# Layer 3 of a four-layer network on one core: one half's products summed by TensorE, the other half's by VectorE, in an order planned without the exclusion of VectorE and GpSimd

## The chip, the core and the metric

The kernel runs on one core of a Trainium2 chip. The metric is the time of one execution in device microseconds (us). A core has a matrix engine (TensorE, PE in the profile; PEld is its weight load), a vector engine (VectorE, DVE), an engine for functions of one input (ScalarE, ACT), a general engine (GpSimd, POOL) and one that issues transfers (SyncE, SP). Each engine works through its own queue in order. Engines wait for one another by semaphores, and an instruction that waits holds up all that stand behind it in its queue. SBUF is the large on-chip memory; PSUM is the small one that TensorE writes, in eight banks of 128 x 512 float32.

## The reference: what is computed

Four layers follow each other on x of 8 x 256 x 32 x 32. The change is in the last one, layer 3, a deformable convolution. Cut to what matters:

```
h = silu(bn(conv2d(x, w_cv1, 3x3)))              # 256 -> 128 channels
t = gelu(layernorm(depthwise3x3(h) + b_dw))
value  = h @ w_inp + b_inp
offset = t @ w_off + b_off                        # 4 groups x 9 taps x (x, y)
mask   = softmax(t @ w_msk + b_msk, over 9 taps)
o = sum over 9 taps of mask * bilinear(value at tap + offset)
out = x + silu(bn(o @ w_out + b_out))
```

As long as no offset is larger than 1, each bilinear sample of a 3 x 3 tap lies in a 5 x 5 window. So o is a sum of 25 products: the value image shifted by (sx, sy), times a weight for every pixel and group. The kernel computes these 25 weights a pixel from offsets and mask, forms the 25 products and adds them.

## The kernel before

Layer 3 works batch by batch, b = 0 to 7, each in two halves h of 512 pixels (16 rows of 32), channels on the 128 partitions. A tile of one half is 128 x 512 float32, one PSUM bank.

The front of a batch: `add_normed` (L1174) finishes the layer ahead of it in x, `border` copies it into a padded image, `convolve3` (L1182) does 18 float32 matmuls a half into one PSUM tile `pc`, `silu` (L1187) puts them in the image `h3`. `values` and `values_copy` make the value image `v3`. `depthwise` (L1205 on ScalarE, then eight multiply-adds in PSUM at L1208 on VectorE) and the layer norm (`centered`, `variances`, `deviations`, `inverse` at L1240, `inverse_spread`, `scaled` at L1250) lead to `gelu`, `offsets3` and `offsets3_add` (L1266). `masks` is the softmax: a maximum, a subtraction (L1300), an exponential on ScalarE, a sum and reciprocal, a multiplication (L1307). `weights` (L1319 to L1325) builds the 25 weights of each pixel in 15 instructions, on GpSimd for b > 0 and on VectorE for b = 0. `parts` (L1334, L1336) splits them into three bfloat16 parts, ScalarE casting and VectorE subtracting; TensorE turns them and ScalarE copies them to `wT`.

The sum of a half, 25 steps s: `shift_weights` (L1355) spreads one step's weights over the channels by a matmul into one of three PSUM tiles `pw`. `product` (L1360) multiplies it by the shifted value image on VectorE into one of six SBUF tiles `pr`. Each product is then added by one of two engines: `add_pe` (L1366) adds it in the PSUM tile `pa` by a matmul with the identity, and `add_pool` (L1372 and L1374) adds it in the SBUF tile `part` on GpSimd. `by_pe` (L1131) gives TensorE steps 1, 5, 9, 13, 17 and 21 for b < 4 and the twelve odd steps up to 23 for b >= 4; GpSimd has the rest. `add_both` (L1377) adds the two sums on VectorE, `outward` (L1381) and `outward_silu` (L1386) are the last matmul and the activation, `add_input` (L1391) adds x on GpSimd, and `store` issues the transfer out.

The order of the work is planned while the program is written out. Every step is a `piece` with an engine, a planned duration, a rank, the pieces it follows, and the rings from which it takes a buffer and to which it gives one back. `Order.run` repeatedly picks, over all engines, the piece that can start first by the planned times, the lower rank on a tie, and emits it. So the plan decides in which order each engine's queue holds the pieces; on the chip only data and buffers are waited for. A ring's buffer comes free 0.15 us after the planned end of the piece that gives it. Front pieces have rank 100 b, convolutions 100 b + 100, products and their adds 100 b + 150.

One ring, `port`, has one entry and no buffer. Every GpSimd piece but one (the clearing of the weights' tile) takes and gives it, and so do the VectorE pieces L1300, L1307 and L1334: in the plan these never overlap a GpSimd piece, and two GpSimd pieces stand at least 0.15 us apart. Planned durations are 0.68 for a product, 0.86 for a TensorE add, 1.25 for a GpSimd add, 0.45 for each of L1300 and L1307, 1.0 for L1334, and 0.75, 2.1 and three times 0.75 for each third of the weights on GpSimd.

Of the kernel before, what the change touches and what calls it, by code (L numbers as in the profile page):

```python
# [8 lines left out]
F32 = mybir.dt.float32  # L9
# [9 lines left out]
P = 128  # L19
# [3 lines left out]
HALF = N // 2  # L23
# [62 lines left out]
def pixels(ap):  # L86
    return ap.rearrange("c (r w) -> c r w", w=W)
# [71 lines left out]
def conv_seq_kernel(ctx: ExitStack, tc: tile.TileContext, d: dict, out: bass.AP):  # L159
    nc = tc.nc  # L160
    x_in = d["x"]
    B = x_in.shape[0]
# [10 lines left out]
    ident = const.tile([P, P], F32, name="ident")  # L173
# [62 lines left out]
    with ExitStack() as s0:  # L236
        w = s0.enter_context(tc.tile_pool(name="a_w", bufs=1))
# [419 lines left out]
    with ExitStack() as s1_:  # L657
# [58 lines left out]
        def piece(key, engine, time, rank, after, f, *args, take=(), give=(), lag=Order.LAG):  # L716
            T[key] = work.add(engine, time, rank, [T[a] for a in after if a in T], lambda: f(*args), take, give, lag)
# [349 lines left out]
    with ExitStack() as s3_:  # L1067
# [55 lines left out]
        def bank3():  # L1123
# [4 lines left out]
        nc.vector.tensor_reduce(group, ident.rearrange("p (g c) -> p g c", c=GC), AX.X, ALU.add)  # L1128


        by_pe = [range(1, 25, 4) if b < 4 else range(1, 25, 2) for b in range(B)]  # L1131
        by_pool = [[s for s in range(25) if s not in by_pe[b]] for b in range(B)]

        work = Order(
            port=1, ld=3, xp0=1, xp1=1, h3=3, v3=2, ln=1, wt=1, wT=2, pr=6, part=2, res=3, spread=2,
            ps=2, pc=1, pd=1, pw=3, pa=1,  # L1140
        )
        T, S = {}, {}

        def piece(key, engine, time, rank, after, f, *args, take=(), give=(), lag=Order.LAG, kind=None, port=False):
            if port:
                take, give = [*take, "port"], [*give, "port"]
            T[key] = work.add(engine, time, rank, [T[a] for a in after if a in T], lambda: f(*args), take, give, lag, kind)

        def cols(h):
# [205 lines left out]
            nc.tensor.matmul(S["pw", b, h, s], sel[: rows(i), r, :], S["wT", b][: rows(i), i, cols(h)], start=True, stop=True)  # L1355

        def product(b, h, s):
            S["pr", b, h, s] = gp.tile([P, HALF], F32, name="pr")
            v = window(v3s[b % 2], s // 5, s % 5, H // 2, h * H // 2)
            nc.vector.tensor_mul(pixels(S["pr", b, h, s]), pixels(S.pop(("pw", b, h, s))), v)  # L1360

        def add_pe(b, h, s):
            on_pe = by_pe[b]
            if s == on_pe[0]:
                S["acc", b, h] = pa.tile([P, HALF], F32, name="pa")
            nc.tensor.matmul(S["acc", b, h], ident, S.pop(("pr", b, h, s)), start=s == on_pe[0], stop=s == on_pe[-1])  # L1366

        def add_pool(b, h, n):
            on_pool = by_pool[b]
            if n == 1:  # L1370
                S["part", b, h] = two.tile([P, HALF], F32, name="part")
                nc.gpsimd.tensor_add(S["part", b, h], S.pop(("pr", b, h, on_pool[0])), S.pop(("pr", b, h, on_pool[1])))  # L1372
            else:
                nc.gpsimd.tensor_add(S["part", b, h], S["part", b, h], S.pop(("pr", b, h, on_pool[n])))  # L1374
# [25 lines left out]
        for b in range(B):  # L1400

            r = 100 * b
            for t in range(2):
                piece(("ld", b, t), "SP", 0.5, r, [], load, b, t, take=["ld"], lag=5.0)
                for h in range(2):
                    piece(("n", b, t, h), "ACT", 0.75, r, [("ld", b, t)], normed3, b, t, h, take=["ps"], give=["ld"] * h)
                    piece(("a", b, t, h), "DVE", 0.68, r, [("n", b, t, h)], add_normed, b, t, h, give=["ps"])
                piece(("xp", b, t), "ACT", 1.08, r, [("a", b, t, 0), ("a", b, t, 1)], border, b, t, take=[f"xp{t}"])
            last = ("c", b - 1, 1, 1, 8)
            for h in range(2):  # L1410
                for t in range(2):
                    for k in range(9):
                        c = b, h, t, k
                        take = ["pc"] if t == k == 0 else []
                        give = [f"xp{t}"] if h == 1 and k == 8 else []
                        piece(("c", *c), "PE", 0.86, r + 100, [("xp", b, t), last], convolve3, *c, take=take, give=give)
                        last = "c", *c
                piece(("si", b, h), "ACT", 0.78, r, [last], silu, b, h, take=["h3"] * (1 - h), give=["pc"], kind="silu")
            for h in range(2):
# [12 lines left out]
            piece(("inv", b), "DVE", 1.74, r, [("dev", b)], inverse, b)  # L1432
            for h in range(2):
                piece(("is", b, h), "PE", 0.86, r, [("inv", b)], inverse_spread, b, h, take=["ps"])
                piece(("sc", b, h), "DVE", 0.68, r, [("is", b, h), ("zc", b, h)], scaled, b, h, give=["ps"])
                piece(("ge", b, h), "ACT", 0.68, r, [("sc", b, h)], gelu, b, h, kind="gelu")
                piece(("o", b, h), "PE", 1.1, r, [("ge", b, h), ("o", b, h - 1)], offsets3, b, h, take=["ps"] + ["wt"] * (1 - h), give=["ln"] * h)
                piece(("oa", b, h), "DVE", 0.6, r, [("o", b, h), ("oa", b, h - 1)], offsets3_add, b, h, give=["ps"])
            om = [("oa", b, 0), ("oa", b, 1)]
            piece(("ms", b, 0), "DVE", 0.7, r, om, masks, b, 0)  # L1440
            piece(("ms", b, 1), "DVE", 0.45, r, [("ms", b, 0)], masks, b, 1, port=True)
            piece(("ms", b, 2), "ACT", 0.44, r, [("ms", b, 1)], masks, b, 2, kind="exp")
            piece(("ms", b, 3), "DVE", 1.0, r, [("ms", b, 2)], masks, b, 3)
            piece(("ms", b, 4), "DVE", 0.45, r, [("ms", b, 3)], masks, b, 4, port=True)
            for i in range(3):
                piece(("ha", b, i), "ACT", 0.67, r, om + [("ha", b, i - 1)], hats, b, i)
            piece(("ha", b, 3), "DVE", 0.72, r + 90, [("ha", b, 0)], hats, b, 3)
# [4 lines left out]
            for i in range(3):  # L1452
                for j in range(-1, 4):
                    time = (0.75, 2.1, 0.75, 0.75, 0.75)[j + 1] if b else (0.4, 1.06, 0.47, 0.47, 0.47)[j + 1]
                    piece(("w", b, i, j), "POOL" if b else "DVE", time, r, ready + last, weights, b, i, j, port=True)
                    last = [("w", b, i, j)]
            for i in range(3):
                piece(("p", b, i, 0), "ACT", 0.86, r, last, parts, b, i, 0)
                last = [("p", b, i, 0)]
                if i < 2:  # L1460
                    piece(("p", b, i, 1), "DVE", 1.0, r, last, parts, b, i, 1, port=True)
                    last = [("p", b, i, 1)]
            for i in range(3):
                piece(("t", b, i), "PE", 1.0, r, last + [("t", b, i - 1)], turned3, b, i, take=["ps"], give=["wt"] if i == 2 else [])
# [2 lines left out]
            r = 100 * b + 150  # L1467
            for h in range(2):
                k = b, h
                for s in range(25):  # L1470
                    last = s == 24 and h == 1
                    before = ("g", *k, s - 1) if s else ("g", b, 0, 24) if h else ("g", b - 1, 1, 24)
                    after = [("tc", b, s // SB), before] + ([("sel", s % SB, 2)] if b == h == 0 else [])
                    piece(("g", *k, s), "PE", 0.25, r, after, shift_weights, *k, s, take=["pw"], give=["wT"] if last else [])
                    piece(("pr", *k, s), "DVE", 0.68, r, [("g", *k, s), ("vc", b, 0), ("vc", b, 1)], product, *k, s, take=["pr"], give=["pw"] + ["v3"] * last)
                on_pe, on_pool = by_pe[b], by_pool[b]
                for s in on_pe:
                    after = [("pr", *k, s)] + ([("ap", *k, s - on_pe.step)] if s > on_pe[0] else [])
                    piece(("ap", *k, s), "PE", 0.86, r, after, add_pe, *k, s, take=["pa"] if s == on_pe[0] else [], give=["pr"])
                for n in range(1, len(on_pool)):  # L1480
                    after = [("pr", *k, on_pool[n])] + [("pr", *k, on_pool[0]) if n == 1 else ("ao", *k, n - 1)]
                    piece(
                        ("ao", *k, n), "POOL", 1.25, r, after, add_pool, *k, n,
                        take=["part"] if n == 1 else [], give=["pr"] * (1 + (n == 1)), port=True,
                    )
                piece(("ab", *k), "DVE", 0.68, r - 100, [("ap", *k, on_pe[-1]), ("ao", *k, len(on_pool) - 1)], add_both, *k, give=["pa"])
                for t in range(2):
                    piece(("ow", *k, t), "PE", 0.86, r - 100, [("ab", *k)], outward, *k, t, take=["ps"], give=["part"] * t)
                    piece(("os", *k, t), "ACT", 0.78, r - 50, [("ow", *k, t)], outward_silu, *k, t, take=["res"], give=["ps"], kind="silu")
                    piece(("oi", *k, t), "POOL", 1.25, r - 100, [("os", *k, t)], add_input, *k, t, port=True)  # L1490
# [6 lines left out]
        ps = bank3()  # L1497
# [248 lines left out]
```

## Time and profile before

| | |
|---|---|
| median of 3 runs | 4257.02 us (4256.65 to 4259.13) |
| the profiled execution | 4256.73 us |
| its span, first to last instruction | 4254.9 us |
| mean granted TensorE clock | 0.977 |
| busy, of the span | PE 93%, DVE 71%, POOL 78%, ACT 44% |
| layer 3's stage, about 3570 to 4255 us | PE 608.3, DVE 470.7, POOL 462.6, ACT 245.2 us busy |
| products of batch 0 to 7 begin at | 3665, 3745, 3818, 3894, 3969, 4052, 4133, 4195 us |
| last convolution of batch 0 to 7 ends at | 3609, 3649, 3710, 3772, 3839, 3902, 3966, 4079 us |

How to read it: the page gives each engine's busy time, the span in 40 slices (each digit the busy share in tenths), and groups of instructions by line of the program, written out<-in with their shapes. In a group, "x400 | 258.0, 683 | 105.7 <-PE pw L1355 61.3" means 400 instructions, busy for 258.0 us, 683 ns each on average, with 105.7 us of idle time of the engine just before them, 61.3 of which were ended by TensorE's `pw`. A row of an order of time gives start, length, the instruction, how many in a row, and in brackets the idle time before it and what ended it. A row of a single line gives shortest, median and longest duration in ns. A row of stretches gives the stretch, its length, each engine's busy time with its number of instructions, the granted clock, and the transfers' share and rate. A float32 matmul stands as two rows in the trace.

### The profile page before, as it was taken

How to read it: one execution, taken by the hardware profiler on the slowest of the kernel's cores; microseconds unless marked ns; L12 is line 12 of the kernel's file. 1: busy time of each engine (PE TensorE's matmuls, PEld its weight loads, DVE VectorE, ACT ScalarE, POOL GpSimd, SP SyncE). 2: the span in 40 equal slices, each digit the busy share in tenths (PEclk: the TensorE clock that was granted, in tenths of full speed). 3: DMA queues.
4: the chain of work that ended last, by engine and by line, in shares of the span. 5: the costliest groups of instructions: out<-in, count | busy, mean ns of one | idle time of the engine just before them, and what ended most of it. 6: DMA issues, size and time to landing. Idle time of an engine off the chain costs nothing.

```text
span 4254.9 us, 60310 instructions
## 1 busy us (share of the span) xinstructions
PE 3972.3 (93%) x20975; PEld 1542.8 (36%) x20975; DVE 3026.9 (71%) x5147; ACT 1858.0 (44%) x3335; POOL 3313.3 (78%) x2023
## 2 busy tenths in 40 slices
PE   6999999999999999999999999898899978999976
PEld 2333333333333333333333333343343333444432
DVE  6767777777777767777677776567777774777665
ACT  2555545545545555555555555332232324443321
POOL 2888889889898898888888889357777771489767
PEclk8999999999999999999999999999999998999998
DMA  5212212212222222122222121134344442000000
GB/s 174 62 54 57 77 50 63 71 50 65 66 56 69 59 59 73 51 65 68 53 60 74 51 62 48 45 99 115 116 120 121 121 132 72 5 11 15 15 15 21
DMA packets 207225, 283.11 MB, mean 67 GB/s; under 512 B 87216, under 2 KB 117440, under 8 KB 206656
## 3 DMA queue, kind: packets, MB, share of 16 engines
q1 hardware_dynamic: 176352, 195.46, 16.2%
q0 software_dynamic: 28720, 77.90, 6.2%
q10 hardware_dynamic: 1840, 5.81, 0.4%
q8 instruction: 169, 2.77, 0.3%
q14 instruction: 144, 1.18, 0.1%
HBM read 181.07 MB, written 63.82 MB: 58 GB/s over the span
## 4 chain that ended last, share of the span: by engine, by line
PE 72%; DVE 13%; POOL 7%; issue 4%; DMA 3%; ACT 2%; SPq 0%; DVEq 0%; POOLq 0%; ACTq 0%
PE av L460 20%; PE pb L403 12%; PE sc L448 11%; PE pb L386 5%; PE pc L1182 5%; POOL g L885 5%; PE pb L534 3%; PE pa L1366 2%; PE pb L330 2%; PE pm L752 2%; PE po L765 2%; DMA g<-table,idx 2%; DVE pm L407 2%; PE pw L1355 2%; DVE r L491 1%
## 5 line engine op out<-in xcount | busy, mean ns | idle before, releaser
L470 POOL TENSOR_TENSOR esum<-esum,e 128x1024 f32<-128x1024 f32 x762 | 1809.0, 2407 | 55.1 <-ACT e L449 54.7
L407 DVE TENSOR_REDUCE pm<-pb 128x1 f32<-128x512 f32 x2016 | 1356.3, 685 | 656.1 <-PE pb L403 652.0
L449 ACT ACTIVATE e<-sc 128x512 f32<-128x512 f32 x2048 | 1056.5, 603 | 677.0 <-PE sc L448 665.7
L460 PE MATMUL av<-e,v 128*64 128x512 f32 x4096 | 1054.2, 593 | 0.0
L403 PE MATMUL pb<-sk,sq 128*64 128x512 bf16 x4032 | 773.2, 387 | 56.3 <-DVE x L542 23.5
L885 POOL DMA_INDIRECT g<-table,idx x576 | 550.4, 955 | 256.4 <-issue 159.0
L403 PEld LDWEIGHTS <-sq 128*64 128x64 bf16 x4032 | 266.7, 109 | 911.5 <-issue 887.0
L448 PE MATMUL sc<-q,k 32*128 32x512 f32 x4096 | 590.6, 641 | 0.0
L468 POOL TENSOR_TENSOR esum<-e 128x1024 f32<-128x1024 f32 x127 | 303.2, 2409 | 298.9 <-ACT e L449 298.9
L460 PEld LDWEIGHTS av<-e,v 128*64 128x64 f32 x4096 | 295.0, 137 | 208.1 <-issue 117.3
L1374 POOL TENSOR_TENSOR part<-part,pr 128x512 f32<-128x512 f32 x224 | 289.4, 1293 | 67.5 <-DVE pr L1360 56.2
L1360 DVE TENSOR_TENSOR pr<-pw,v 128x512 f32<-128x512 f32 x400 | 258.0, 683 | 105.7 <-PE pw L1355 61.3
L1182 PE MATMUL pc<-xpad,wc 128*128 128x512 f32 x576 | 279.0, 611 | 4.1 <-ACT h L1187 4.1
L448 PEld LDWEIGHTS sc<-q,k 32*128 32x128 f32 x4096 | 164.6, 183 | 229.8 <-issue 185.6
L534 PE MATMUL pb<-o,wp 128*64 128x512 f32 x1024 | 244.3, 596 | 1.4 <-DVE r L512 1.2
L752 PE MATMUL pm<-y,wide 128*128 128x512 f32 x512 | 237.9, 609 | 6.1 <-DVE y L726 5.7
L386 PE MATMUL pb<-wide,y 128*64 128x256 f32 x2048 | 241.8, 379 | 0.0
L765 PE MATMUL po<-hid,w 128*128 128x512 f32 x512 | 239.7, 615 | 1.8 <-DVE x L769 1.7
L491 DVE RECIPROCAL r<-r 128x128 f32<-128x128 f32 x252 | 237.1, 942 | 0.1
L390 ACT COPY v<-pb 128x512 f32<-128x512 f32 x128 | 74.9, 585 | 266.0 <-PE pb L386 266.0
L907 DVE TENSOR_TENSOR near_p<-g,near_p 128x320 f32<-128x320 f32 (+1 forms) x384 | 177.3, 462 | 13.2
L911 DVE TENSOR_TENSOR samp<-samp,near_p 128x320 f32<-128x320 f32 (+1 forms) x384 | 174.0, 453 | 13.2
(256 smaller groups left out, 3893.7 us busy)
## 6 DMA issues: line engine op xcount, KB each, us to landing
sq<-lev_d SPq DMA_DIRECT2D x512, 64.0 KB
r<-r SPq DMA_DIRECT2D x504, 64.0 KB
sk<-lev_d SPq DMA_DIRECT2D x496, 64.0 KB
lev_d<-lev SPq DMA_DIRECT2D x180, 128.0 KB
u_d<-u SPq DMA_DIRECT2D x60, 256.0 KB
g<-table,idx POOLq DMA_INDIRECT x576, 2.7
table<-v SPq DMA_DIRECT2D x32, 256.0 KB
out<-res SPq DMA_DIRECT2D x32, 256.0 KB
```

Source lines behind the costliest of these rows:

```text
L386: nc.tensor.matmul(ps[c * 64 : (c + 1) * 64, (mt % 2) * 256 : (mt % 2 + 1) * 256], ys[b][:, t, k0 : k0 + 64], wv[:, t, g * 256 : (g + 1) * ...
L403: nc.tensor.matmul(ps[c * 64 : (c + 1) * 64, :], sq[pair][:, c, q0 : q0 + 64], sk[pair][:, c, kh * HALF : (kh + 1) * HALF], start=True, st ...
L407: nc.vector.tensor_reduce(maxima[m][:, pair, qt, kh : kh + 1], ps, AX.X, ALU.max)
L448: nc.tensor.matmul(ps, k[r, kt * P : (kt + 1) * P], q[r, h * HALF : (h + 1) * HALF], start=True, stop=True)
L449: nc.scalar.activation(es[m, kt, j // 2][:, j % 2, :], ps, AF.Exp)
L460: nc.tensor.matmul(av[i * HD : (i + 1) * HD, :], vss[b, g][:, kt, j * HD : (j + 1) * HD], e[:, i, :], start=kt == 0, stop=kt == NT - 1,)
L470: eng.tensor_add(sums[m, pair], sums[m, pair], es.pop((m, kt, pair)))
L534: nc.tensor.matmul(ps[c * 64 : (c + 1) * 64, :], wp[:, 2 * g + i, o0 : o0 + 64], outs[(b, g, h), i], start=i == 0, stop=i == 1,)
L752: nc.tensor.matmul(ps, w1[:, t, i * P : (i + 1) * P], ys[b, h][:, t, :], start=t == 0, stop=t == 1)
L765: nc.tensor.matmul(pss["o", b, h, t], w2[:, j, t * P : (t + 1) * P], hids[b, h, j], start=j == 0, stop=j == 7)
L885: nc.gpsimd.indirect_dma_start(out=g[:, k, :], out_offset=None, in_=tables[b][:TR, :], in_offset=bass.IndirectOffsetOnAxis(ap=idxs[b][:, t ...
L1182: nc.tensor.matmul(S["c", b, h], wc[:, t, k, :], tap(xpads[t], k, H // 2, h * H // 2), start=t == k == 0, stop=t == 1 and k == 8,)
```

## The change

It touches layer 3 alone.

- For batches 0 to 5 the first half's products are summed by TensorE (8 of 25) and GpSimd (17), the second half's by VectorE (10) and GpSimd (15). For batches 6 and 7 TensorE has 12 in both halves, as before.
- In a half that VectorE helps, the first helped product (step 1) is written straight into the PSUM tile `pa`, which it takes then, and nine more are added to it by VectorE in place, one float32 tensor_tensor each.
- The ring `port` is gone. The planned durations of L1300 and L1307 become 0.8, that of L1334 becomes 1.7.
- The VectorE pieces L1174, L1250 and L1266 get rank r - 500; VectorE's adds have one less than the products' rank. The convolution's rank, `r + 100`, is written `100 * b + 100`, which is the same number there.

The diff, cut where a line only loses `port=True`:

```diff
-        by_pe = [range(1, 25, 4) if b < 4 else range(1, 25, 2) for b in range(B)]
-        by_pool = [[s for s in range(25) if s not in by_pe[b]] for b in range(B)]
+        HELP = [("PE", 8), ("DVE", 10)] * 6 + [("PE", 12)] * 4
+        helper = {(b, h): HELP[2 * b + h][0] for b in range(B) for h in range(2)}
+        helped = {(b, h): [(2 * i + 1) * 25 // (2 * HELP[2 * b + h][1]) for i in range(HELP[2 * b + h][1])] for b in range(B) for h in range(2)}
+        by_pool = {k: [s for s in range(25) if s not in helped[k]] for k in helped}
...
         work = Order(
-            port=1, ld=3, xp0=1, xp1=1, h3=3, v3=2, ln=1, wt=1, wT=2, pr=6, part=2, res=3, spread=2,
+            ld=3, xp0=1, xp1=1, h3=3, v3=2, ln=1, wt=1, wT=2, pr=6, part=2, res=3, spread=2,
             ps=2, pc=1, pd=1, pw=3, pa=1,
         )
...
-            if port:
-                take, give = [*take, "port"], [*give, "port"]
...
         def product(b, h, s):
-            S["pr", b, h, s] = gp.tile([P, HALF], F32, name="pr")
+            on = helped[b, h]
+            if s == on[0] and helper[b, h] == "DVE":
+                dst = S["acc", b, h] = pa.tile([P, HALF], F32, name="pa")
+            else:
+                dst = S["pr", b, h, s] = gp.tile([P, HALF], F32, name="pr")
             v = window(v3s[b % 2], s // 5, s % 5, H // 2, h * H // 2)
-            nc.vector.tensor_mul(pixels(S["pr", b, h, s]), pixels(S.pop(("pw", b, h, s))), v)
-
-        def add_pe(b, h, s):
-            on_pe = by_pe[b]
-            if s == on_pe[0]:
+            nc.vector.tensor_mul(pixels(dst), pixels(S.pop(("pw", b, h, s))), v)
+
+        def add_helper(b, h, s):
+            on = helped[b, h]
+            if helper[b, h] == "DVE":
+                nc.vector.tensor_add(S["acc", b, h], S["acc", b, h], S.pop(("pr", b, h, s)))
+                return
+            if s == on[0]:
                 S["acc", b, h] = pa.tile([P, HALF], F32, name="pa")
-            nc.tensor.matmul(S["acc", b, h], ident, S.pop(("pr", b, h, s)), start=s == on_pe[0], stop=s == on_pe[-1])
+            nc.tensor.matmul(S["acc", b, h], ident, S.pop(("pr", b, h, s)), start=s == on[0], stop=s == on[-1])
...
-                    piece(("a", b, t, h), "DVE", 0.68, r, [("n", b, t, h)], add_normed, b, t, h, give=["ps"])
+                    piece(("a", b, t, h), "DVE", 0.68, r - 500, [("n", b, t, h)], add_normed, b, t, h, give=["ps"])
...
-                        piece(("c", *c), "PE", 0.86, r + 100, [("xp", b, t), last], convolve3, *c, take=take, give=give)
+                        piece(("c", *c), "PE", 0.86, 100 * b + 100, [("xp", b, t), last], convolve3, *c, take=take, give=give)
...
-                piece(("sc", b, h), "DVE", 0.68, r, [("is", b, h), ("zc", b, h)], scaled, b, h, give=["ps"])
+                piece(("sc", b, h), "DVE", 0.68, r - 500, [("is", b, h), ("zc", b, h)], scaled, b, h, give=["ps"])
...
-                piece(("oa", b, h), "DVE", 0.6, r, [("o", b, h), ("oa", b, h - 1)], offsets3_add, b, h, give=["ps"])
+                piece(("oa", b, h), "DVE", 0.6, r - 500, [("o", b, h), ("oa", b, h - 1)], offsets3_add, b, h, give=["ps"])
...
-            piece(("ms", b, 1), "DVE", 0.45, r, [("ms", b, 0)], masks, b, 1, port=True)
+            piece(("ms", b, 1), "DVE", 0.8, r, [("ms", b, 0)], masks, b, 1)
...
-            piece(("ms", b, 4), "DVE", 0.45, r, [("ms", b, 3)], masks, b, 4, port=True)
+            piece(("ms", b, 4), "DVE", 0.8, r, [("ms", b, 3)], masks, b, 4)
...
-                    piece(("p", b, i, 1), "DVE", 1.0, r, last, parts, b, i, 1, port=True)
+                    piece(("p", b, i, 1), "DVE", 1.7, r, last, parts, b, i, 1)
...
-                    piece(("pr", *k, s), "DVE", 0.68, r, [("g", *k, s), ("vc", b, 0), ("vc", b, 1)], product, *k, s, take=["pr"], give=["pw"] + ["v3"] * last)
-                on_pe, on_pool = by_pe[b], by_pool[b]
-                for s in on_pe:
-                    after = [("pr", *k, s)] + ([("ap", *k, s - on_pe.step)] if s > on_pe[0] else [])
-                    piece(("ap", *k, s), "PE", 0.86, r, after, add_pe, *k, s, take=["pa"] if s == on_pe[0] else [], give=["pr"])
+                    piece(
+                        ("pr", *k, s), "DVE", 0.68, r, [("g", *k, s), ("vc", b, 0), ("vc", b, 1)], product, *k, s,
+                        take=["pa" if dve and s == on[0] else "pr"], give=["pw"] + ["v3"] * last,
+                    )
+                for i, s in list(enumerate(on))[dve:]:
+                    after = [("pr", *k, s)] + ([("ap" if i > dve else "pr", *k, on[i - 1])] if i else [])
+                    piece(
+                        ("ap", *k, s), "DVE" if dve else "PE", 0.7 if dve else 0.86, r - dve, after, add_helper, *k, s,
+                        take=[] if dve or s > on[0] else ["pa"], give=["pr"],
+                    )
```

More of the change, by code (lines that the diff above doesn't have):

```diff
@@ L1142, in conv_seq_kernel, with piece @@
         T, S = {}, {}
-        def piece(key, engine, time, rank, after, f, *args, take=(), give=(), lag=Order.LAG, kind=None, port=False):
-            if port:
-                take, give = [*take, "port"], [*give, "port"]
+        def piece(key, engine, time, rank, after, f, *args, take=(), give=(), lag=Order.LAG, kind=None):
             T[key] = work.add(engine, time, rank, [T[a] for a in after if a in T], lambda: f(*args), take, give, lag, kind)
@@ L1357, in product @@
         def product(b, h, s):
-            S["pr", b, h, s] = gp.tile([P, HALF], F32, name="pr")
-            v = window(v3s[b % 2], s // 5, s % 5, H // 2, h * H // 2)
-            nc.vector.tensor_mul(pixels(S["pr", b, h, s]), pixels(S.pop(("pw", b, h, s))), v)
-        def add_pe(b, h, s):
-            on_pe = by_pe[b]
-            if s == on_pe[0]:
+            on = helped[b, h]
[3 more added lines that the diff above has]
+                dst = S["pr", b, h, s] = gp.tile([P, HALF], F32, name="pr")
+            v = window(v3s[b % 2], s // 5, s % 5, H // 2, h * H // 2)
+            nc.vector.tensor_mul(pixels(dst), pixels(S.pop(("pw", b, h, s))), v)
[5 more added lines that the diff above has]
+            if s == on[0]:
                 S["acc", b, h] = pa.tile([P, HALF], F32, name="pa")
-            nc.tensor.matmul(S["acc", b, h], ident, S.pop(("pr", b, h, s)), start=s == on_pe[0], stop=s == on_pe[-1])
+            nc.tensor.matmul(S["acc", b, h], ident, S.pop(("pr", b, h, s)), start=s == on[0], stop=s == on[-1])
         def add_pool(b, h, n):
-            on_pool = by_pool[b]
+            on_pool = by_pool[b, h]
             if n == 1:
@@ L1454, in conv_seq_kernel @@
                     time = (0.75, 2.1, 0.75, 0.75, 0.75)[j + 1] if b else (0.4, 1.06, 0.47, 0.47, 0.47)[j + 1]
-                    piece(("w", b, i, j), "POOL" if b else "DVE", time, r, ready + last, weights, b, i, j, port=True)
+                    piece(("w", b, i, j), "POOL" if b else "DVE", time, r, ready + last, weights, b, i, j)
                     last = [("w", b, i, j)]
@@ L1469, in conv_seq_kernel @@
                 k = b, h
+                on, on_pool, dve = helped[k], by_pool[k], helper[k] == "DVE"
                 for s in range(25):
@@ L1483, in conv_seq_kernel @@
                         ("ao", *k, n), "POOL", 1.25, r, after, add_pool, *k, n,
-                        take=["part"] if n == 1 else [], give=["pr"] * (1 + (n == 1)), port=True,
+                        take=["part"] if n == 1 else [], give=["pr"] * (1 + (n == 1)),
                     )
-                piece(("ab", *k), "DVE", 0.68, r - 100, [("ap", *k, on_pe[-1]), ("ao", *k, len(on_pool) - 1)], add_both, *k, give=["pa"])
+                piece(("ab", *k), "DVE", 0.68, r - 100, [("ap", *k, on[-1]), ("ao", *k, len(on_pool) - 1)], add_both, *k, give=["pa"])
                 for t in range(2):
@@ L1489, in conv_seq_kernel @@
                     piece(("os", *k, t), "ACT", 0.78, r - 50, [("ow", *k, t)], outward_silu, *k, t, take=["res"], give=["ps"], kind="silu")
-                    piece(("oi", *k, t), "POOL", 1.25, r - 100, [("os", *k, t)], add_input, *k, t, port=True)
+                    piece(("oi", *k, t), "POOL", 1.25, r - 100, [("os", *k, t)], add_input, *k, t)
                     piece(("st", *k, t), "SP", 0.5, r, [("oi", *k, t)], store, *k, t, give=["res"])
```

## The prediction

> **What bounds the kernel now.** First the page's slices, to see which part of the run the change can touch. Its stage is the last 685 us (3570 to 4255); nothing ahead of it is edited.
>
> ```profile
> PE   6999999999999999999999999898899978999976
> ...
> POOL 2888889889898898888888889357777771489767
> ```
>
> TensorE is full at the stage's start and GpSimd (POOL) nearly so; in its last third neither is. Next the stretches. I cut them where a batch's first product (the multiply at L1360) begins, so each row is one batch's 50 products, with whatever work for later batches runs beside them.
>
> ```profile
> core 0: us, PE busy (x) PEld busy (x) DVE busy (x) ACT busy (x) POOL busy (x), PEclk, DMA share, GB/s
> 3665.30:3744.60 79.30, 77.52 (x247) 32.99 (x248) 56.53 (x84) 28.55 (x37) 64.89 (x54) 1.00 0.02 7
> 3744.60:3817.80 73.20, 70.92 (x236) 32.34 (x236) 57.23 (x87) 32.91 (x39) 63.85 (x54) 0.95 0.04 15
> 3817.80:3893.80 76.00, 74.44 (x236) 32.73 (x235) 57.78 (x88) 31.07 (x40) 67.90 (x57) 1.00 0.04 15
> 3893.80:3969.20 75.40, 74.03 (x235) 33.02 (x234) 55.52 (x83) 29.62 (x36) 69.81 (x58) 1.00 0.04 15
> 3969.20:4052.00 82.80, 72.98 (x223) 30.86 (x223) 55.25 (x86) 27.19 (x33) 54.07 (x47) 0.92 0.04 13
> 4052.00:4133.40 81.40, 61.20 (x183) 25.11 (x182) 50.57 (x76) 20.97 (x27) 51.63 (x44) 0.90 0.04 14
> ```
>
> In batches 0 to 3 TensorE is at 97 to 98%, but part of that is convolution (L1182) run ahead of need: 340 matmul rows fall in these 303.9 us where four batches need 288. The 52 extra are 26 matmuls, at 163.77 us / 170 = 0.96 us each 25 us, which leaves (296.9 - 25) / 4 = 68 us of TensorE per batch. GpSimd has 64 to 70 of 73 to 76 us in batches 1 to 3, and VectorE 57. So two engines are near the limit and the third has some 18 us to spare. Batches 4 and 5 are the longest, and yet no engine is full: they wait on one another. The rows of VectorE's order of time in batch 4 show how.
>
> ```profile
> 3984.56 2.57 DVE L1360 TENSOR_TENSOR pr<-pw,v 128x512 f32<-128x512 f32 x4
> ...
> 4003.54 2.04 DVE L1360 TENSOR_TENSOR pr<-pw,v 128x512 f32<-128x512 f32 x3 [10.66 <-POOL part L1374]
> 4009.08 1.75 DVE L1240 RECIPROCAL rs<-rs 128x256 f32<-128x256 f32 x1 [3.50 <-ACT rs L1237]
> 4016.42 1.29 DVE L1250 TENSOR_TENSOR wide<-ps,wide 128x512 f32<-128x512 f32 x2 [5.59 <-PE ps L1246]
> ```
>
> The 10.66 us are a full ring: six product buffers, all held for GpSimd, which builds the next batch's sampling weights (L1319 to L1325, 15 instructions from 3984.8 to 4002.3, with one other of 1.26 us among them) and sums nothing meanwhile. Last the durations, from the groups and the single lines.
>
> ```profile
> L1366 PE MATMUL pa<-pr,ident 128*128 128x512 f32 x288 | 156.4, 625 | 2.9 <-DVE pr L1360 2.7
> L1374 POOL TENSOR_TENSOR part<-part,pr x224: 1257/1267/1903, 3668.7 to 4237.1; 128x512 f32<-128x512 f32 x112
> 3714.07 23.41 POOL L1374 TENSOR_TENSOR part<-part,pr 128x512 f32<-128x512 f32 x17
> 4080.93 5.50 DVE L1208 SCALAR_TENSOR_TENSOR pd<-h,vec,pd 128x512 f32<-128x512 f32 x7 [7.19 <-ACT pd L1205]
> L1300 DVE TENSOR_TENSOR mask<-om,top x8: 448/470/1285, 3637.4 to 4139.5; 128x288 f32<-128x288 f32 x8
> L1307 DVE TENSOR_TENSOR mask<-mask,top x8: 447/449/459, 3640.8 to 4144.9; 128x288 f32<-128x288 f32 x8
> L1334 DVE TENSOR_TENSOR ws<-ws,parts x16: 980/1134/1932, 3653.4 to 4170.8; 128x800 f32<-128x800 f32 x16
> ```
>
> GpSimd's adds take 1.27 us but follow each other every 23.41 / 17 = 1.38. Two of the last three rows have a tail: their longest takes 0.8 to 0.95 us more than their shortest.
>
> **The change, part by part.** One execution is the base: 4256.73 us, its span 4254.9 and 1.8 around it; the median shown is 0.3 above.
>
> *TensorE's adds.* 144 become 96: in batches 0 to 3 both halves had 6, now one has 8 and the other none (4 fewer a batch); in 4 and 5 both had 12 (16 fewer); in 6 and 7 nothing changes. An add is two rows. In a full queue it takes 0.86 us start to start (one at 4057.82, the next matmul at 4058.68); by the group it is 156.4 / 144 = 1.09. So TensorE loses 3.4 us a batch in 0 to 3 and 13.8 in 4 and 5, 41 us in all (52 by the group). Beside it lies run-ahead convolution, so the time is not shortened by all of this.
>
> *GpSimd's adds.* 36 a batch become 30 (16 + 14) in 0 to 3, and 24 become 30 in 4 and 5. At 1.38 that is -8.3 us a batch, then +8.3; 12 adds or 16.6 us fewer in all.
>
> *VectorE's adds.* Nine a batch in 0 to 5, 54 new ones; the tenth product of a helped half goes straight into the PSUM sum. No row before adds in place in PSUM with tensor_tensor. Below, products in a row start (2.57 - 0.68) / 3 = 0.63 us apart; above, the chain at L1208, also in place in PSUM, has (5.50 - 0.75) / 6 = 0.79. The chain is the nearest row; its instruction by itself is 0.07 longer (754 ns) than a tensor_tensor (681), so I take 0.72: 6.5 us a batch, 39 in all, between 34 and 43. Queued behind such an add are the next products, and behind them TensorE's next window matmul, which needs the buffer that a product gives back. The first product of the second half must now wait until the sum of the first half is read (L1377), because the PSUM buffer is one; three window buffers let only two later products pass it. Before, TensorE's first add had the same wait and the product did not. In the trace that read ends 4 us after the last product of batch 0's first half and 24 us after batch 1's, so I price this from 0 to 2 us a batch, and take 1: GpSimd's shorter sum makes the lag shorter.
>
> *No exclusion in the plan.* It issues no wait now and none before; it only ordered. Without it four VectorE instructions a batch (L1300, L1307, twice L1334) can meet a GpSimd add. A meeting costs up to 1285 - 448 = 0.84 us at L1300 and 1932 - 980 = 0.95 at L1334; today's means are 0.63, 0.45 and 1.28. From none to all met that is 0 to 0.65 + 0.83 + 2 x 0.65 = 2.8 us a batch on VectorE, and the tail of L1374 (1903 against 1257) says as much for GpSimd. Less than nothing is excluded for L1307, already at its floor; the others could win back 0.8. With GpSimd busy for four fifths of a batch I take 1.5 on each engine.
>
> The Trainium skill (SBUF — State Buffer, section Who interferes with whom) speaks against this part: a VectorE instruction with two inputs in SBUF and a GpSimd one that reads SBUF exclude each other for a whole instruction. These rows look like that, and by the rule each meeting would cost up to a whole add, 1.27 us, 5 us a batch. The same rule spares the new PSUM adds, with one SBUF input; no row here can show it.
>
> *Ranks.* The VectorE steps that empty a bank (L1174, L1250, L1266) go ahead of others ready at the same time. They are 8 a batch of 0.6 to 0.7 us; at most one other instruction of 0.7 is passed each time. I take nothing; it lies beside the products of another batch, and without that cover it is worth 1 us either way. The convolution's rank is the same number written otherwise. DMAs, SP's included, keep their number and follow what they followed.
>
> *Sum.* After it, a middle batch (1 to 3) needs on TensorE 68 - 3.4 = 64.6; on GpSimd 67.2 (the three rows' mean) - 8.3 + 1.5 = 60.4; on VectorE 56.8 + 6.5 + 1 + 1.5 = 65.8. The largest falls from 68 to 65.8, but three engines are now level and each has less room to make up a wait. I take 2 us a batch for 0 to 3: 8. In batches 4 and 5 TensorE has 13.8 less, GpSimd 62 and 60, VectorE 64 and 59. These are loads of a middle batch, so I give them its present length, 74.9, and some more for the weights' stall that stays: 77. That is 82.8 + 81.4 - 154 = 10. Batches 6 and 7 keep their work and begin earlier; the front of batch 7 ends on TensorE's convolution, which gains as much. Together -18: 4256.73 - 18 = 4238.7, forecast 4239.
>
> **The rivals.** *GpSimd late against its plan (slower).* The planner prices an add at 1.25; before, the exclusion put 0.15 between any two, so 1.40, above the real 1.38. Now it believes 1.25, and every VectorE and TensorE instruction behind a buffer that GpSimd gives back stands 0.13 too early in its queue. Thirty adds a batch make 3.9 us, the weights' chain (planned 15.3, now 17.5 - 1.26 = 16.2) 0.9 more: 4.8, at worst 5 x 6 = 30 us, and TensorE stays filled but with the wrong work. For it: VectorE already waits 10.66 and 9.8 us for GpSimd at such places. Against it: GpSimd has 60 us of work in a batch of 74, so the plan's lead is caught up whenever it runs dry. It decides from 3 us a batch, where it eats the 18; at its worst 4257 - 18 + 30 = 4269, and with no gain from the new split 4287.
>
> *Meetings eat it (no change).* All four instructions met in six batches, both engines: 2 x 2.8 x 6 = 34 of engine time, half of it on the path, 17: 4256. For it, the tails above; against, most of them stand in the next batch's front, which has slack.
>
> *The gain is whole.* If every batch from 0 to 5 runs as near its largest engine as the trace's best one (73.2 against 70.92, a factor 1.03), six of 65.8 x 1.03 + 1 = 69 replace 468.1: 4257 - 54 = 4203. Against it: level engines wait more.
>
> **How the numbers follow.** The forecast (4215 to 4248) has 0.41, the whole gain 0.09, meetings or nothing 0.14, GpSimd's lag or VectorE as the bound 0.36. What a measurement can tell is 0.2%, 8.5 us. Faster 0.50, same 0.14, slower 0.36. The range goes from the whole gain, 4203, to the lag without a gain, 4287.
>
> **What would show it.** 96 adds at L1366's successor and 54 VectorE adds in PSUM of 0.68 to 0.76 us; VectorE at 85 to 90% in batches 0 to 3, GpSimd down to some 60 us; batches 4 and 5 at 77 us or less; masks and L1334's successor nearer 0.65 and 1.6 us. I am wrong if VectorE's idle time before products grows with GpSimd as its releaser, if batches 0 to 3 become longer than 76 us, or if one of the last two does.

## The result, and the profile after

The changed kernel takes 4230.96 us (median of 4 runs) against 4256.84 us before: a ratio of 0.9938, 95% interval 0.9923 to 0.9953, or 26 us less. The profiled execution took 4232.61 us, its span is 4230.8.

The stretches of the changed kernel, cut again where a batch's first product begins (columns as before: stretch, its length, then busy time of PE, PEld, DVE, ACT and POOL, the granted clock, transfers):

```profile
3670.30:3745.80 75.50, 72.16 (x232) 31.39 (x232) 61.85 (x92) 27.24 (x34) 57.99 (x48) 1.00 0.02 7
3745.80:3820.30 74.50, 72.76 (x254) 32.73 (x253) 66.88 (x98) 34.85 (x44) 61.20 (x51) 1.00 0.04 15
3820.30:3890.50 70.20, 66.49 (x218) 29.39 (x217) 61.50 (x93) 28.33 (x36) 60.50 (x50) 1.00 0.04 16
3890.50:3968.10 77.60, 67.87 (x216) 29.49 (x215) 61.60 (x92) 30.42 (x38) 59.11 (x50) 0.93 0.04 14
3968.10:4039.30 71.20, 65.06 (x209) 29.10 (x208) 61.09 (x93) 25.07 (x32) 60.47 (x50) 0.95 0.04 15
4039.30:4110.50 71.20, 50.09 (x139) 18.66 (x138) 61.56 (x92) 22.76 (x29) 59.45 (x50) 0.69 0.04 15
4110.50:4170.50 60.00, 44.79 (x132) 16.54 (x131) 39.12 (x61) 12.90 (x15) 51.97 (x43) 0.85 0.05 18
4170.50:4214.20 43.70, 39.23 (x107) 13.55 (x105) 34.12 (x54) 3.11 (x4) 36.53 (x29) 1.00 0.07 24
```

Batches 0 to 3 take 297.8 us in place of 303.9, batches 4 and 5 together 142.4 in place of 164.2, batches 6 and 7 together 103.7 in place of 105.7. From the first product to the end of the last batch it is 543.9 in place of 573.8; I call this length the stage of products below. Against these 29.9 us stands a first product that starts 5 us later in this execution; 3.2 of these are there at the masks of batch 0 already. VectorE is busy for 374 of the 440 us of batches 0 to 5, where it had 333 of 468; its idle time there fell from 135 to 66 us.

The groups and single lines of the changed kernel (L1369 is the new add, L1373 TensorE's, L1381 GpSimd's; a single line has shortest, median and longest duration):

```profile
L1373 PE MATMUL pa<-pr,ident 128*128 128x512 f32 x192 | 107.2, 641 | 2.1 <-DVE pr L1364 2.1
L1381 POOL TENSOR_TENSOR part<-part,pr 128x512 f32<-128x512 f32 x212 | 275.8, 1301 | 55.6 <-DVE pr L1364 44.6
L1369 DVE TENSOR_TENSOR pa<-pa,pr x54: 685/700/700, 3718.3 to 4108.2; 128x512 f32<-128x512 f32 x54
L1300 DVE TENSOR_TENSOR mask<-om,top x8: 457/782/1233, 3640.6 to 4110.1; 128x288 f32<-128x288 f32 x8
L1307 DVE TENSOR_TENSOR mask<-mask,top x8: 457/553/1476, 3644.6 to 4114.7; 128x288 f32<-128x288 f32 x8
L1334 DVE TENSOR_TENSOR ws<-ws,parts x16: 983/1451/1971, 3655.4 to 4142.5; 128x800 f32<-128x800 f32 x16
```

The 54 adds cost 0.70 us each. The masks and the parts' subtraction are longer, as an order without the exclusion would have it. VectorE's idle time before products with GpSimd as its releaser is 33.7 us in all, where it was 38.9 (28.4 before L1374's and 10.5 before L1372's release).

### The profile page after: what moved, and what is told of

Same layout as the page of the kernel before. It is cut to its first block, busy times and chain, and to the rows that moved or that the text cites. A ratio compares the mean times of both kernels' runs of the same rounds, so it can differ in the third digit from the quotient of the medians.

```text
span 4230.8 us, 60121 instructions
## 1 busy us (share of the span) xinstructions
PE 3943.3 (93%) x20879; PEld 1529.8 (36%) x20879; DVE 3069.4 (73%) x5201; ACT 1853.5 (44%) x3332; POOL 3299.0 (78%) x2011
## 4 chain that ended last, share of the span: by engine, by line
PE 67%; DVE 13%; POOL 10%; issue 5%; DMA 3%; ACT 1%; SPq 0%; DVEq 0%; POOLq 0%; ACTq 0%
PE av L460 20%; PE pb L403 12%; PE sc L448 11%; POOL g L885 6%; PE pb L386 5%; PE pc L1182 4%; PE pb L534 3%; DMA g<-table,idx 2%; PE pb L330 2%; PE pm L752 2%; POOL part L1381 2%; PE po L765 2%; DVE pm L407 2%; DVE r L491 2%; PE pb L481 1%
## 5 line engine op out<-in xcount | busy, mean ns | idle before, releaser
L1381 POOL TENSOR_TENSOR part<-part,pr 128x512 f32<-128x512 f32 x212 | 275.8, 1301 | 55.6 <-DVE pr L1364 44.6
L1364 DVE TENSOR_TENSOR pr<-pw,v 128x512 f32<-128x512 f32 x394 | 253.7, 682 | 62.1 <-POOL part L1381 33.7
L1182 PE MATMUL pc<-xpad,wc 128*128 128x512 f32 x576 | 276.6, 605 | 5.3 <-ACT h L1187 5.3
```

The lines of the kernel that those rows point to most:

```text
L1182: nc.tensor.matmul(S["c", b, h], wc[:, t, k, :], tap(xpads[t], k, H // 2, h * H // 2), start=t == k == 0, stop=t == 1 and k == 8,)
```

## The experiments

All times are medians; the kernel before took 4256.8 to 4258.1 us beside them, except in the last one. "Division" is which engine adds which products, "order" is the rest of the change.

**The division alone.**

```diff
 work = Order(
+    port=1, ld=3, xp0=1, xp1=1, h3=3, v3=2, ln=1, wt=1, wT=2, pr=6, ...
 ...   # port=True, 0.45 and 1.0, rank r: all as before
 HELP = [("PE", 8), ("DVE", 10)] * 6 + [("PE", 12)] * 4
```

> The new division of the sums alone: the plan keeps the exclusion ring, the old planned durations and the old ranks. Theory S (the gain of 26 us comes from the division, which takes load from GpSimd in batches 0 to 3 and from TensorE in 4 and 5): 4225 to 4238 us, and batches 4 and 5 of 68 to 74 us each in place of 83 and 81. Theory O (the gain comes from the order that the plan finds without the exclusion and with the new ranks): 4246 to 4260, batches 4 and 5 still of 78 or more.

4259.03 us, ratio 1.0001 (0.9992 to 1.001): nothing is gained. GpSimd is relieved in batches 0 to 3 (57 to 62 us, where it had 64 to 70), and yet batches 2 and 3 take 88 us each; in each of them one product waits for GpSimd, by 9.3 and 10.8 us. Theory S falls in its plain form.

**The order alone.**

```diff
-HELP = [("PE", 8), ("DVE", 10)] * 6 + [("PE", 12)] * 4
+HELP = [("PE", 6)] * 8 + [("PE", 12)] * 8     # with the old steps
```

> The order alone: no exclusion ring, the new planned durations and ranks, but TensorE has its old steps (6 of 25 in batches 0 to 3, 12 from 4 on) and VectorE adds none. Theory S: 4250 to 4266, no gain, with the masks and the parts' subtraction longer by some 0.3 us each. Theory O: 4228 to 4242.

4274.37 us, ratio 1.004 (1.0027 to 1.0054): 17 us lost. So neither part has the gain, and both together have it. Theory O falls too. This order has no exclusion, and yet three products in it wait long for GpSimd, by 14.6, 10.8 and 11.3 us in batches 2, 4 and 5.

**The new division in batches 4 and 5 only, and in 0 to 3 only**, the new order in both.

```diff
-HELP = [("PE", 8), ("DVE", 10)] * 6 + [("PE", 12)] * 4
+HELP = [("PE", 6)] * 8 + [("PE", 8), ("DVE", 10)] * 2 + [("PE", 12)] * 4   # 4 and 5; 6 with the old steps
+HELP = [("PE", 8), ("DVE", 10)] * 4 + [("PE", 12)] * 8                     # 0 to 3
```

> The changed kernel, but batches 0 to 3 keep the old division (TensorE 6 of 25 in both halves, VectorE none). By the forecast's terms (8 us from batches 0 to 3, 10 from 4 and 5) it loses about half of the gain: 4241 to 4247. By the stretches of the trace after (6 us from 0 to 3, 22 from 4 and 5) it keeps most of it: 4233 to 4240.

> The changed kernel, but batches 4 and 5 keep the old division (TensorE 12 of 25 in both halves, VectorE none). By the forecast's terms 4240 to 4248; by the stretches of the trace after 4246 to 4254, with batches 4 and 5 of 78 us or more, and VectorE idle again behind GpSimd's weights for 10 us at a time.

4246.9 us (ratio 0.9976, 0.9966 to 0.9985) and 4242.89 us (0.9966, 0.9954 to 0.9978). Measured from the order alone, the new division is worth 27 us in batches 4 and 5, 31 us in 0 to 3, and 43 us in all six. The first lies at the edge of the forecast's terms, the second within them. Batches 4 and 5 took 76.5 and 77.8 us with the old division, below the 78 expected and well below the 82.8 and 81.4 of before: part of what looked like their relief comes from the order. The length of one batch has to be read with care, though: with the ranks alone (below) batches 4 and 5 take 77.4 and 75.5 us and batch 3 takes 84.6 where it took 75.4, and the whole gains nothing. Time can move from one batch to its neighbours.

**A GpSimd add planned at its real distance.**

```diff
-("ao", *k, n), "POOL", 1.25, r, after, add_pool, *k, n,
+("ao", *k, n), "POOL", 1.38, r, after, add_pool, *k, n,
```

> The changed kernel with one number of the plan altered: a GpSimd add is planned at 1.38 us, the distance at which these adds follow each other in the trace before, and not at 1.25. If the plan's lead over GpSimd costs the changed kernel what the rival on it said (up to 5 us a batch), 4205 to 4222. If the lead is caught up whenever GpSimd runs dry, 4226 to 4236, and VectorE's waits for GpSimd stay where they were.

4242.11 us, 0.9963 (0.995 to 0.9977): 11 us slower than the changed kernel, which neither expectation had. A truer plan gave a worse order, with three long waits of products for GpSimd (8.8, 11.7 and 11.5 us) where the changed kernel has two. The rival of a GpSimd that falls behind its plan has nothing for it here.

**The exclusion put back into the changed kernel**; division and new ranks stay.

```diff
-    ld=3, xp0=1, xp1=1, h3=3, ...
+    port=1, ld=3, xp0=1, xp1=1, h3=3, ...
-piece(("ms", b, 1), "DVE", 0.8, r, ...)
+piece(("ms", b, 1), "DVE", 0.45, r, ..., port=True)    # and its like
```

> The changed kernel with the exclusion ring and its planned durations put back (0.45 and 1.0); the division and the new ranks stay. If meetings of VectorE and GpSimd cost what the forecast took (1.5 us a batch on each engine) and it lies on the path: 4219 to 4227, with the masks back at 0.46 us and the parts' subtraction nearer 1.0. If meetings lie beside other work: 4228 to 4235. If the ring's 0.15 us between GpSimd pieces makes a worse order: 4236 to 4250.

4266.6 us, 1.0019 (1.001 to 1.0028): 36 us slower than the changed kernel, more than any expectation. The exclusion does what it is for. Its masks and its parts' subtraction (lines are two further down there):

```profile
L1302 DVE TENSOR_TENSOR mask<-om,top x8: 447/458/467, 3640.1 to 4145.5; 128x288 f32<-128x288 f32 x8
L1309 DVE TENSOR_TENSOR mask<-mask,top x8: 446/448/610, 3643.5 to 4163.3; 128x288 f32<-128x288 f32 x8
L1336 DVE TENSOR_TENSOR ws<-ws,parts x16: 977/985/1743, 3656.2 to 4190.9; 128x800 f32<-128x800 f32 x16
```

That saves little, and the loss stands elsewhere: its batches 3, 4 and 5, with no engine full (TensorE at 88% in batch 3, below that everywhere else).

```profile
3885.90:3978.20 92.30, 81.64 (x235) 33.84 (x236) 62.40 (x96) 30.03 (x38) 62.52 (x53) 0.96 0.05 17
3978.20:4061.00 82.80, 64.03 (x170) 24.09 (x170) 59.73 (x92) 25.34 (x32) 57.59 (x48) 0.81 0.02 7
4061.00:4140.70 79.70, 46.94 (x157) 19.61 (x157) 56.86 (x87) 22.69 (x30) 58.50 (x51) 0.73 0.04 14
```

In VectorE's order of time each of these three has one product that waits for GpSimd, by 10.33, 9.2 and 10.1 us. The first of them:

```profile
3927.60 1.54 DVE L1210 SCALAR_TENSOR_TENSOR pd<-h,vec,pd 128x512 f32<-128x512 f32 x2
3939.47 0.69 DVE L1366 TENSOR_TENSOR pr<-pw,v 128x512 f32<-128x512 f32 x1 [10.33 <-POOL part L1383]
3940.08 0.75 DVE L1210 SCALAR_TENSOR_TENSOR pd<-h,vec,pd 128x512 f32<-128x512 f32 x1
```

The product waits for a buffer of the ring, all six of which are held. Behind it in the queue stand the last steps of the next batch's depthwise convolution, which need no product buffer and wait all the same; the whole front of that batch is held up with them. This made the theory for the last runs: what the change moves is where VectorE's queue stands when the product ring is full.

**The new division in batches 6 and 7 too.**

```diff
-HELP = [("PE", 8), ("DVE", 10)] * 6 + [("PE", 12)] * 4
+HELP = [("PE", 8), ("DVE", 10)] * 8
```

> The changed kernel with the new division in batches 6 and 7 too (TensorE 8 and VectorE 10 in place of TensorE 12 and 12). If TensorE, busy for 39 of batch 7's 44 us, sets the end: 4222 to 4228. By loads alone, a first half then has 16 GpSimd adds of 1.38 = 22 us and a second half 25 x 0.63 + 9 x 0.70 = 22 us on VectorE, against 21 to 22 us a half now: 4230 to 4236.

4243.97 us, 0.9969 (0.9958 to 0.998): 13 us slower than the changed kernel, the loss larger than the loads said. Its batches 6 and 7:

```profile
4109.00:4174.30 65.30, 38.77 (x101) 12.44 (x100) 45.15 (x71) 12.89 (x15) 59.58 (x49) 0.71 0.04 17
4174.30:4223.90 49.60, 34.18 (x72) 9.73 (x71) 39.49 (x63) 3.11 (x4) 44.00 (x35) 0.74 0.06 21
```

With the convolutions done, GpSimd has 44.0 of batch 7's 49.6 us, where it had 36.5 of 43.7. There TensorE's twelve adds were the better use.

**The three ranks alone, in the kernel before.**

```diff
-piece(("a", b, t, h), "DVE", 0.68, r, [("n", b, t, h)], ...)
+piece(("a", b, t, h), "DVE", 0.68, r - 500, [("n", b, t, h)], ...)    # and sc, oa
```

> The kernel before with the three new ranks (r - 500 at L1174, L1250, L1266) and nothing else. The forecast took nothing for them: 4251 to 4262. Theory O in its narrow form (the ranks carry the gain): 4230 to 4245.

4255.63 us, 0.9996 (0.9987 to 1.0005): no difference that can be told.

**Ten product buffers, the changed kernel's order.** The plan still counts six, so each queue keeps its sequence (one small reduction at the end of the layer moves); only waits for a product buffer go.

```diff
-gp = s3_.enter_context(tc.tile_pool(name="d_g", bufs=6))
+gp = s3_.enter_context(tc.tile_pool(name="d_g", bufs=10))     # pr=6 in Order stays
```

> The changed kernel's own order, planned with six product buffers, but ten of them on the chip: every queue holds the same instructions in the same sequence, and only the waits for a product buffer get looser. VectorE's two waits of 10 us for GpSimd (at 3919 and 4138 us in the trace after) and its shorter ones make 34 us of the stage. If these waits for the ring are on the path: 4208 to 4222. If they lie beside GpSimd's weights, which have to be done anyway: 4226 to 4233.

4223.44 us, 0.992 (0.9907 to 0.9934), the fastest of all: 7.5 us below the changed kernel, between the two expectations. VectorE in batch 3, first of the changed kernel, then of this one:

```profile
3906.31 3.12 DVE L1208 SCALAR_TENSOR_TENSOR pd<-h,vec,pd 128x512 f32<-128x512 f32 x4
3919.49 0.69 DVE L1364 TENSOR_TENSOR pr<-pw,v 128x512 f32<-128x512 f32 x1 [10.05 <-POOL part L1381]
3920.09 0.75 DVE L1208 SCALAR_TENSOR_TENSOR pd<-h,vec,pd 128x512 f32<-128x512 f32 x1
```

```profile
3906.96 3.12 DVE L1208 SCALAR_TENSOR_TENSOR pd<-h,vec,pd 128x512 f32<-128x512 f32 x4
3909.99 0.68 DVE L1364 TENSOR_TENSOR pr<-pw,v 128x512 f32<-128x512 f32 x1
3910.59 0.75 DVE L1208 SCALAR_TENSOR_TENSOR pd<-h,vec,pd 128x512 f32<-128x512 f32 x1
```

The same queue, without the wait; batch 3 falls from 77.6 to 69.8 us. The other long wait of the changed kernel, 11.5 us in batch 6, gave next to nothing back (60.0 to 59.2 us): with ten buffers VectorE waits there for the parts of the weights, 11.0 us, which have to come anyway. So of these two waits the one with other work queued behind it cost time.

**Ten product buffers, the order with the exclusion put back.**

```diff
 # the exclusion put back, as above
-gp = s3_.enter_context(tc.tile_pool(name="d_g", bufs=6))
+gp = s3_.enter_context(tc.tile_pool(name="d_g", bufs=10))
```

> The kernel with the exclusion put back into the changed one (4266.6 us), its order untouched, with ten product buffers on the chip in place of six. If the exclusion costs time because its order leaves VectorE waiting for the product ring (30 us in all in its trace, in five long waits), those waits go and the time falls towards the changed kernel's: 4232 to 4248. If the order itself holds every queue back, whatever the ring: 4258 to 4268.

4235.3 us, 0.9947 (0.9934 to 0.9961): 31 of the 36 us that the exclusion cost are back, with every queue's sequence unchanged. VectorE's waits of products for GpSimd (total, times, longest), with six buffers and with ten; those for TensorE's `pw` stay (39.5 and 41.8 us):

```profile
DVE pr L1366 <- POOL part L1383: 30.5, 5, 10.3
```

```profile
DVE pr L1366 <- POOL part L1383: 2.6, 3, 1.2
```

So most of what the order with the exclusion loses, it loses at the ring. Not all: with ten buffers each it is still 12 us behind the changed order (4235.3 against 4223.44 us).

**The order alone, with the real pace of GpSimd in its plan.**

```diff
 # the order alone, as above
-("ao", *k, n), "POOL", 1.25, r, after, add_pool, *k, n,
+("ao", *k, n), "POOL", 1.38, r, after, add_pool, *k, n,
```

> The order alone with the old division (4274.4 us), with the GpSimd adds planned at 1.38 us, their real distance, in place of 1.25. If its loss comes from GpSimd falling behind the plan, which has next to no slack for it with 36 adds a batch: 4245 to 4260. If not: 4268 to 4280, or any number on either side by a chance of order.

4267.34 us, 1.0021 (1.0012 to 1.003): 7 us better, not within either range. Its products wait 41 us for GpSimd as before. The step is in the rival's direction but half of the least that it asked for, so the lag is at most a part of what makes the order alone slow.

**Ten product buffers, the order of the kernel before.**

```diff
 # in the kernel before
-gp = s3_.enter_context(tc.tile_pool(name="d_g", bufs=6))
+gp = s3_.enter_context(tc.tile_pool(name="d_g", bufs=10))
```

> The kernel before, its order untouched, with ten product buffers on the chip in place of six. Its trace has three waits of about 10 us of VectorE for the ring (at 4003, 4073 and 4168 us) and small ones. If the waits for the ring are what the changed kernel got rid of: 4226 to 4238, near the changed kernel's 4231. If the ring matters only in the orders planned for the new division, where VectorE has little room: 4246 to 4258.

This run's chip was slower for both kernels (4568.95 against 4589.13 us), ahead of layer 3: the first product starts at 3994.5 us. The ratio is 0.9954 (0.9939 to 0.997), 20 us. On the 4257 us of the other chips that ratio would give 4237, an estimate, at the upper end of the first range and outside the second. The stage of products, on the trace, is 548.1 us, 25.7 less than before with six; the six-buffer trace comes from another chip, but batch 0 takes 79.3 us in both. Its batches 4 and 5, and what its products waited for GpSimd:

```profile
4296.50:4365.60 69.10, 68.77 (x224) 30.05 (x223) 55.24 (x85) 27.19 (x33) 55.54 (x47) 1.00 0.04 16
4365.60:4437.10 71.50, 59.43 (x183) 24.48 (x183) 50.41 (x75) 21.02 (x27) 51.78 (x44) 0.93 0.04 15
```

```profile
DVE pr L1360 <- POOL part L1374: 1.3, 2, 0.9
```

Together 140.6 us, below the changed kernel's 142.4: what the change gained in batches 4 and 5 can be had with the old division, the old order and four more buffers.

What a wait for the ring holds up need not stand in VectorE's queue. Behind the product that waited 10.66 us in batch 4 of the kernel before stand two more products and a reciprocal whose input is not there yet. But that product gives back a window buffer, and TensorE waits for it; behind in TensorE's queue stand the next batch's `variances` (L1231) and convolution (L1182). TensorE before:

```profile
4004.29 0.59 PE L1355 MATMUL pw<-wT,sel 120*128 120x512 bf16 x1 [9.49 <-DVE pr L1360]
4008.97 6.36 PE L1182 MATMUL pc<-xpad,wc 128*128 128x512 f32 x10
```

The same ten rows of convolution with ten buffers:

```profile
4324.40 4.57 PE L1182 MATMUL pc<-xpad,wc 128*128 128x512 f32 x10
```

So the wait cost twice: TensorE stood idle, and the 11.1 us from 4004.2 on ran at a granted clock of 0.62, where with ten buffers the 7 us from 4322.0 on ran at 1.00.

The stage of products of the three orders, with six buffers and with ten:

| order | six | ten | the ring's share |
|---|---|---|---|
| before | 573.8 us | 548.1 us | 25.7 |
| the change with the exclusion put back | 579.0 | 552.2 | 26.8 |
| the change | 543.9 | 536.1 | 7.8 |

The first row is taken from two chips; on the chip of its ten-buffer run the whole times differ by 20 us. In the second row the whole time falls by 31 us, 5 of them ahead of the first product.

Of the 29.9 us between the first and the last row, 12.0 remain with ten buffers in both; the other 17.9 are what the ring of six costs the old order more than the changed one. It is not that the changed order waits much less for the ring (33.7 us against 38.9, above): its waits cost less. In the first and second row the two orders with the exclusion lose about alike at the ring, whatever the division. And with ten buffers the new division has no gain over the old one as long as both plans have the exclusion: 552.2 against 548.1 us, with ratios to the kernel before of 0.9947 and 0.9954, which can't be told apart. What remains, 0.992, came only without the exclusion. The order alone (no exclusion, old division) was not run with ten buffers, so whether that rest needs the new division too is not known.

## Why the prediction was right, and where its reason was not

The time (forecast -17.8 us, measured -25.9) and the direction are right. That the sum came so near is in part luck: its reason, lower loads, gains nothing by itself (the division alone), and its largest term, batches 4 and 5, came true by another cause. By its steps:

- TensorE's adds: -41 to -52 us of busy time; measured 156.4 - 107.2 = 49. GpSimd's adds: 16.6 us fewer at 1.38 us from start to start; in busy time, without the distance between them, measured 289.4 - 275.8 = 13.6. VectorE's: 0.72 us each between 0.63 and 0.79, 39 in all; measured 0.70 and 37.7. These terms hold.
- Waiting for the sum's PSUM buffer: 1 us a batch. The wait for GpSimd at the sum of a half is 7.7 us over all in the trace after, against 2.1 before, 0.9 for each of six batches.
- Meetings: 1.5 us a batch on each of VectorE and GpSimd. The three lines' mean durations rose from 0.634, 0.451 and 1.276 to 0.799, 0.758 and 1.364 us, 5.2 us over eight batches or 0.65 a batch; GpSimd's add by 0.008 us, 0.24 a batch of 30. So the price was more than twice too high on VectorE and several times on GpSimd. What the Trainium skill (SBUF — State Buffer, section Who interferes with whom) says of instructions with one input in SBUF agrees with the PSUM adds: they stay between 0.685 and 0.700 us, though 49 of the 54 ran beside a GpSimd instruction. The price that the prediction drew from that page, up to a whole add for each meeting and 5 us a batch, was far above the 0.65 measured.
- Batches 0 to 3: forecast -8, measured -6.1, with the load as it was worked out (VectorE 85% busy on average, GpSimd 58 to 61 us). One of the prediction's signs of being wrong did come up: batch 3 took 77.6 us, over the 76 that it named (the mean of the four is 74.5), by the wait of 10.05 us for the ring. Batches 4 and 5: forecast -10, measured -21.8. This is the term that was mis-sized, and the step that failed is "some more for the weights' stall that stays: 77". The stall was seen, a full ring of six buffers for 10.66 us, and taken as given; it was what mattered. In the changed kernel neither batch 4 nor 5 has a wait of that kind, and without it the old division and order run the two in 140.6 us. Of the 29.9 us, 17.9 are the ring's.
- The reason as a whole, that the largest engine's load falls and so the batch gets shorter, is half right. The largest load did fall, but the division alone relieves the same loads and gains nothing; with the exclusion in its plan it stalls at the ring instead. The forecast took the part on the exclusion for a small cost, and with the new division it decides the sign (4266.6 us with it, 4230.96 without).
- The rival of a lagging GpSimd was not borne out: the truer plan made the changed kernel 11 us slower, and the order alone 7 us faster, less than the rival asked for. The meetings as a rival were too small. The rival of a whole gain (4203) was not reached, since the waits among level engines stayed: VectorE is idle for 7.6 to 16.0 us in each of batches 0 to 5.

What stays open: why some planned orders meet the full ring with other work queued behind it. With the new division the exclusion makes such an order; it spaces GpSimd's pieces and holds three VectorE lines back, and which of the two does it was not tried. But the exclusion is not the only way there, since the order alone has none and has three long waits too. Nor was it shown that the changed order loses less at the ring for a reason and not by chance: one planned duration altered by 0.13 us cost it 11 us.

## What to carry to other kernels

When no engine is full, look first for one wait of many us with independent work queued behind it, in its own queue or in one that it feeds, and at the ring it waits for; here the engine loads alone made no gain. Loosening only the ring on the chip, with the planned order kept, tells in one run how much of a slow order's loss is want of buffers; here four more buffers were worth 8 to 27 us of the stage, depending on the order. Two parts of a change whose effects come through the order of queues cannot be priced one by one: here 0 and +17 made -26.

## What the runs showed of the hardware

An add in place in PSUM on VectorE (128 x 512 float32, one input in SBUF) takes 0.70 us, against 0.68 for the same add out of PSUM into SBUF, and none of 54 was longer than that, though GpSimd worked beside 49 of them. Where the change leaves TensorE idle, its granted clock falls: 0.69 in batch 5 (50 of 71 us busy) where it was 0.90 before (61 of 81 us busy), and a window matmul (L1355) there takes 496 ns on average in place of 394. How much of the relief that takes back was not measured.
